# Layer 0 and 1 of a four-layer graph network: products for two output tiles interleaved with the building of the weights, or one output tile at a time, and layer 2 on the same PSUM banks

## The chip, the cores and the metric

The kernel runs on one core of a Trainium2 chip. The metric is the device time of one execution in microseconds. A profile of one execution is beside it: PE is the matrix engine (TensorE), PEld its weight loads, DVE the vector engine, ACT the scalar engine, POOL the GpSimd engine, SP the engine that issues most of the loads.

## The reference

Sixteen graphs of 1024 nodes with 256 features go through four layers. Each layer normalizes the nodes, applies relu, runs a graph layer on the dense 1024 x 1024 adjacency and adds the result to its input. Layer 0 takes its softmax over axis 1, so over the source rows of the weight matrix; layer 1 over axis 2; layer 2 is a mean over neighbours; layer 3 has four heads of width 64.

```python
# layer 0
h = relu(layernorm(x)) @ W
e = leaky_relu(f1[:, :, None] + f2[:, None, :], 0.2)
attention = softmax(where(adj > 0, e, -9e15), axis=1)
x = x + elu(attention @ h)
# layer 1: the same with softmax over axis -1, and f1, f2 from other weights
# layer 2
msg = einsum('bij,biu->bju', adj, h @ W_msg)
x = x + relu(h @ W_upd + msg / deg + bias)
# layer 3: four heads, edge types, softmax over axis -1, relu, a norm over each head
```

## The kernel before, in words

The graph's 1024 nodes are eight tiles of 128 (NT = 8, P = 128). The adjacency is kept as a mask of bytes, written by ACT at line 557 from loads of SP. Most of the matmuls are plain f32; layer 2 takes the adjacency as it is (fp32r) and splits its other operand in a high and a low part (lines 797 and 798), which go through two matmuls (806 and 807).

**Layer 0.** Eight projections (line 632, put out of PSUM by ACT at line 689), then a front of eight steps: in step j DVE makes the weight tile p of 128 x 1024 with two instructions (lines 710 and 712, the second also sums the row into z), a reciprocal (713), and ACT scales the projected tile j by 1/z (714). Then, for each of the eight output tiles i, PE adds up eight products (line 702, called from two places), ACT takes an exp and a copy of it out of PSUM (727 and 729), and DVE adds the result to x (679 and 680). Each second tile also starts the sums for the next layer's norm: shift on DVE (600), hn and squares on ACT (604 and 609), 1/std on POOL (572 and 573), transposes on PE (626) and a copy to ht on ACT (627).

**Early products.** In this kernel the front of layer 0 also takes two of the eight output tiles with it: two PSUM tiles are taken ahead of it, and each step j adds product j to both. Layer 1 does the same (line 751); its front has one DVE instruction a step (758).

**Layer 2.** For each output tile, 16 matmuls add up in one PSUM tile; ACT scales it out of PSUM (812) and copies the degree (813), DVE adds the update term (814) and adds to x (680). The adjacency is loaded from POOL in four blocks of 256 columns through two buffers (565).

**Layer 3** builds its weights on DVE (847) and accumulates on PE (853) in two PSUM tiles for a head, which DVE takes out (861 and 862). A tail on DVE, POOL and ACT (lines 873 to 895) ends the graph.

**PSUM.** There are four pools of two banks each: tr_ps for transposes, mm_ps for projections, at_ps for the output tiles of layers 0 and 1, hd_ps for the output tiles of layer 2 and the heads of layer 3.

**What sets the order.** The graphs are Python generators. Each yields an estimated length after each step, and a queue sorted by due time runs them, the graphs 120 units apart, so that the source traces some two graphs interleaved. A scheduler then orders the instructions of each engine by what is ready by its own estimates and by the free buffers; [...] In the program so ordered, layer 0 of a graph runs beside layer 2 of the graph before it, and layer 1 beside layer 3 of the graph before it.

## Time and profile before

| what | value |
|---|---|
| median of 3 runs | 2985.34 us (2982.68 to 2987.22) |
| the profiled execution | 2987.22 us |
| its span | 2985.3 us |
| PE, PEld busy | 2600.0, 2049.3 us |
| DVE, ACT, POOL busy | 2037.0, 1353.1, 488.4 us |
| line 702 on PE | 2048 rows, 495.5 us |
| line 751 on PE | 2048 rows, 524.1 us |
| lines 806 and 807 on PE | 1024 rows each, 276.3 and 270.8 us |
| mean granted clock of PE | 0.952 |

The span runs from the first to the last instruction. Busy times are sums over an engine's rows; [...] The chain of work that ended last is followed back from the last instruction, at each step to what released it. The stretches quoted below are of one graph's period in the middle of the run, about 1400 to 1582 us.

### The profile page before, as it was taken

Reading aid. Unit: us, or ns where it says so; the run is one execution under the profiler, and the core shown is the slowest. Engines: PE = TensorE matmul, PEld = TensorE weight load, DVE = VectorE, ACT = ScalarE, POOL = GpSimd, SP = SyncE. Lnnn points to the kernel's source line nnn. Section 1 sums busy time; section 2 is a strip of 40 time slices with the busy share of each in tenths; the row PEclk is TensorE's granted clock in tenths of the full one; section 3 lists DMA queues with packets and bytes.
Section 4 is the critical chain, followed back from the end, with each engine's and each line's share of the span. In section 5 each row is a group of like instructions: output and inputs, shape, how many; then the busy total and the mean of one; then the engine's idle time right before and its main releaser. Section 6 shows DMA issues by size and latency. Waiting matters only on the chain.

```text
span 2985.3 us, 62510 instructions
## 1 busy us (share of the span) xinstructions
PE 2600.0 (87%) x25682; PEld 2049.3 (69%) x25682; DVE 2037.0 (68%) x4054; ACT 1353.1 (45%) x3809; POOL 488.4 (16%) x678
## 2 busy tenths in 40 slices
PE   3899898997989979898898989979899798989974
PEld 2767586775767757577676867757677575876754
DVE  3358566686666867667676776867668675776858
ACT  4453554534445444554535544344554435545340
POOL 1010212102121021211202111021211202111011
PEclk8899999999999999999999999999999999999997
DMA  7021321313223131231413223131231313222120
GB/s 229 22 71 37 116 73 62 100 58 108 63 72 99 62 103 51 90 88 62 110 38 113 72 70 94 63 116 51 86 86 66 99 51 100 79 69 78 38 57 31
DMA packets 146070, 233.71 MB, mean 78 GB/s; under 512 B 9392, under 2 KB 94512, under 8 KB 145776
## 3 DMA queue, kind: packets, MB, share of 16 engines
q1 hardware_dynamic: 74608, 145.73, 14.6%
q0 software_dynamic: 71168, 83.89, 11.1%
q8 instruction: 205, 3.36, 0.5%
q14 instruction: 89, 0.73, 0.1%
HBM read 212.35 MB, written 17.24 MB: 77 GB/s over the span
## 4 chain that ended last, share of the span: by engine, by line
PE 49%; DVE 23%; ACT 9%; DMA 7%; issue 6%; POOL 6%; SPq 0%; ACTq 0%; POOLq 0%; DVEq 0%
PE ps_proj L632 14%; PE ps_o L702 12%; PE ps_o L853 11%; PE ps_o L751 7%; DVE p L710 5%; POOL rs L573 5%; DVE p L712 5%; DVE p L847 4%; DMA raw<-in_adj_t 3%; PE pt_h L626 3%; DMA xs<-in_x 3%; ACT mask L557 3%; DVE p L758 2%; ACT hn L604 1%; DVE xs L680 1%
## 5 line engine op out<-in xcount | busy, mean ns | idle before, releaser
L632 PE MATMUL ps_proj<-wx,ht 128*128 128x258 f32 (+2 forms) x2048 | 686.4, 473 | 46.7 <-DVE up L799 34.4
L847 DVE SCALAR_TENSOR_TENSOR p<-row,q,mask 128x1024 f32<-128x1024 f32 x512 | 639.3, 1277 | 71.6 <-PE ps_o L853 46.6
L853 PEld LDWEIGHTS ps_o<-hb,p 128*64 128x64 f32 x16384 | 514.2, 138 | 128.0 <-issue 62.0
L853 PE MATMUL ps_o<-hb,p 128*64 128x65 f32 x16384 | 569.4, 225 | 13.2 <-DVE p L847 7.3
L751 PE MATMUL ps_o<-hs,p 128*128 128x257 f32 x2048 | 524.1, 398 | 41.6 <-DVE p L758 34.6
L702 PE MATMUL ps_o<-hs,p 128*128 128x256 f32 x2048 | 495.5, 387 | 50.6 <-ACT hs L714 40.2
L632 PEld LDWEIGHTS ps_proj<-wx,ht 128*128 128x128 f32 x2048 | 383.2, 203 | 222.8 <-issue 148.6
L702 PEld LDWEIGHTS ps_o<-hs,p 128*128 128x128 f32 x2048 | 378.4, 192 | 119.9 <-ACT hs L714 53.1
L751 PEld LDWEIGHTS ps_o<-hs,p 128*128 128x128 f32 x2048 | 374.8, 194 | 113.5 <-issue 58.3
L572 POOL TENSOR_SCALAR rs<-sq 128x2 f32<-128x2 f32 x192 | 74.2, 387 | 1856.1 <-ACT unread L609 1839.5
L626 PE MATMUL pt_h<-ident,hn 128*128 128x128 f32 x1024 | 189.3, 301 | 141.1 <-ACT hn L604 133.8
L573 POOL TENSOR_TENSOR rs<-rs,neg_half 128x2 f32<-128x2 f32 (+1 forms) x288 | 309.1, 1084 | 16.1
L604 ACT ACTIVATE hn<-xs,shift 128x256 f32<-128x256 f32 x512 | 240.7, 501 | 142.2 <-DVE shift L600 109.9
L807 PE MATMUL ps_o<-lo,adj 128*128 128x258 f32 x1024 | 270.8, 301 | 31.5 <-DVE lo L798 31.5
L774 ACT ACTIVATE e<-ps_o,shares 128x256 f32<-128x256 f32 x128 | 60.0, 469 | 500.2 <-DVE shares L772 500.1
L806 PE MATMUL ps_o<-hi,adj 128*128 128x258 f32 x1024 | 276.3, 306 | 7.6 <-DMA adj<-in_adj 4.3
L626 PEld LDWEIGHTS pt_h<-ident,hn 128*128 128x128 f32 x1024 | 128.1, 151 | 222.2 <-ACT hn L604 164.4
L807 PEld LDWEIGHTS ps_o<-lo,adj 128*128 128x128 f32 x1024 | 196.9, 193 | 43.3 <-DVE lo L798 35.3
L679 DVE SCALAR_TENSOR_TENSOR xs<-e,xs 128x256 f32<-128x256 f32 x256 | 107.8, 421 | 159.3 <-ACT e L727 136.8
L806 PEld LDWEIGHTS ps_o<-hi,adj 128*128 128x128 f32 x1024 | 196.0, 192 | 25.7 <-issue 14.3
L557 ACT ACTIVATE mask<-raw 128x512 uint8<-128x512 int32 x256 | 160.3, 629 | 109.1 <-DVE p L847 64.5
L889 DVE TENSOR_TENSOR res<-res,rs 128x1024 f32<-128x1024 f32 x32 | 39.2, 1225 | 242.3 <-POOL rs L573 242.3
(91 smaller groups left out, 2735.5 us busy)
## 6 DMA issues: line engine op xcount, KB each, us to landing
raw<-in_adj_t SPq DMA_DIRECT2D x256, 256.0 KB
adj<-in_adj POOLq DMA_DIRECT2D x64, 1024.0 KB, 5.9
row<-d_row SPq DMA_DIRECT2D x112, 512.0 KB
xs<-in_x POOLq DMA_DIRECT2D x32, 512.0 KB, 6.1
out<-res SPq DMA_DIRECT2D x32, 512.0 KB
wx<-in_w SPq DMA_DIRECT2D x3, 256.0 KB
d_row<-e_row SPq DMA_DIRECT2D x48, 4.0 KB
wts<-in_w_t SPq DMA_DIRECT2D x2, 256.0 KB
```

The lines of the kernel that those rows point to most:

```text
L557: nc.scalar.activation(self.bytes[:, n, g * HALF : (g + 1) * HALF], raw, AF.Square, accum_out=squares[:, k : k + 1])
L573: nc.gpsimd.tensor_tensor(rs[:, :n], rs[:, :n], neg_half[:, :n], op=OP.pow)
L604: nc.scalar.activation(hn, xs[:, 2 * g + k, :], AF.Relu, bias=shift[:, k : k + 1])
L626: nc.tensor.transpose(pt[:, c, k * P : (k + 1) * P], hn[:, c * P : (c + 1) * P], ident)
L632: nc.tensor.matmul(ps[:, :width], norm.ht[:, c, n * P : (n + 1) * P], wx[:, c, :width], start=(c == 0), stop=(c == DC - 1))
L702: nc.tensor.matmul(ps[:, :D], ps_[j][:, i * P : (i + 1) * P], hs[:, j, :D], start=(j == 0), stop=(j == NT - 1))
L710: nc.vector.scalar_tensor_tensor(p, row_a, q[:, j : j + 1], row_b, op0=OP.mult, op1=OP.max)
L751: nc.tensor.matmul(ps[:, : D + 1], ps_[j][:, i * P : (i + 1) * P], hs[:, j, : D + 1], start=(j == 0), stop=(j == NT - 1))
L806: nc.tensor.matmul(ps[:, : D + 2], a, hi[:, i, : D + 2], start=(i == 0), stop=False)
L807: nc.tensor.matmul(ps[:, : D + 2], a, lo[:, i, : D + 2], start=False, stop=(i == NT - 1))
L847: nc.vector.scalar_tensor_tensor(p, row, q[:, j, h : h + 1], mask[:, j, :], op0=OP.max, op1=OP.mult)
L853: nc.tensor.matmul(pss[g][part, k * HW : (k + 1) * HW], p[:, i * P : (i + 1) * P][:, part], hbv[:, j, h, :], start=(j == 0 and k == 0), st ...
```

## The change

Layers 0 and 1 no longer take two output tiles along their fronts. All output tiles are written as one loop after the front, eight products to a tile, each tile in a PSUM tile of at_ps. Layer 2 takes its PSUM tiles from at_ps in place of hd_ps. Nothing else differs: the same products are added in the same order within each output tile.

```diff
-    EARLY = 2
...
         ps_ = []
-        early = [at_ps.tile([P, HALF], F32, tag="at", name="ps_o0") for _ in range(EARLY)]
-
-        def product(ps, i, j):
-            nc.tensor.matmul(
-                ps[:, :D], ps_[j][:, i * P : (i + 1) * P], hs[:, j, :D], start=(j == 0), stop=(j == NT - 1)
-            )
-
         for j in range(NT):
...
             ps_.append(p)
-            for i, ps in enumerate(early):
-                product(ps, i, j)
             yield 2.6
         for i in range(NT):
-            if i < EARLY:
-                ps = early[i]
-            else:
-                ps = at_ps.tile([P, HALF], F32, tag="at", name="ps_o0")
-                for j in range(NT):
-                    product(ps, i, j)
+            ps = at_ps.tile([P, HALF], F32, tag="at", name="ps_o0")
+            for j in range(NT):
+                nc.tensor.matmul(
+                    ps[:, :D], ps_[j][:, i * P : (i + 1) * P], hs[:, j, :D], start=(j == 0), stop=(j == NT - 1)
+                )
...
```

Layer 1 is changed in the same way (its products are 257 wide and go to ps_o1). In layer 2:

```diff
-            ps = hd_ps.tile([P, HALF], F32, tag="hd", name="ps_o2")
+            ps = at_ps.tile([P, HALF], F32, tag="at", name="ps_o2")
```

## The prediction

> **What bounds the kernel now.** I read the page first: the engines' shares, then the chain that ended last.

> ```profile
> span 2985.3 us, 62510 instructions
> PE 2600.0 (87%) x25682; PEld 2049.3 (69%) x25682; DVE 2037.0 (68%) x4054; ACT 1353.1 (45%) x3809; POOL 488.4 (16%) x678
> ...
> PE 49%; DVE 23%; ACT 9%; DMA 7%; issue 6%; POOL 6%; SPq 0%; ACTq 0%; POOLq 0%; DVEq 0%
> ```

> No engine bounds the whole. The chain goes to and fro between PE (half of it) and the others, so a move is priced where it lands. PE line 702 (layer 0's products) holds 12% of the chain, 11.5% in the finer chain listing: about 340 us, 21 us for each of 16 graphs. Next I took the chain in order of time. The same piece (ACT v L776) comes back at 1417.49 and 1599.68 us: one graph costs 182.2 us. Then I cut one such period into stages by busy time (columns: stretch, its length, then PE, weight loads, DVE, ACT and POOL busy; granted clock, DMA share, GB/s).

> ```profile
> 1455.70:1479.60 23.90, 21.31 (x138) 18.52 (x136) 23.32 (x51) 10.87 (x32) 5.75 (x7) 1.00 0.54 132
> 1479.60:1512.30 32.70, 32.35 (x164) 27.33 (x164) 15.72 (x47) 22.15 (x71) 6.43 (x12) 1.00 0.24 65
> ```

> The first stretch is layer 0's front: DVE builds the eight weight tiles p (lines 710, 712) and is busy 23.32 of 23.90 us. PE's work there is beside the path. The second is the rest of layer 0, and PE is busy 32.35 of 32.70. The chain of this place shows the hand-over (columns: start, us, what):

> ```profile
> 1477.71 1.16 DVE p L712 x2
> 1478.87 0.02 issue
> 1478.89 0.17 DVE z L713
> 1479.07 0.02 issue
> 1479.09 0.52 ACT hs L714
> 1479.61 0.04 issue
> 1479.65 0.71 PE ps_o L702 x2
> 1480.36 0.02 issue
> 1480.38 0.38 ACT e L727
> 1480.77 0.27 ACT v L729
> 1481.04 0.04 issue
> 1481.08 0.70 PE ps_o L702 x2
> 1481.78 0.12 PE ps_o L806
> 1481.90 0.12 PE ps_o L807
> ...
> 1494.46 3.45 PE ps_o L702 x16
> ```

> Until 1478.89 the chain is DVE's. From 1479.65 it is PE's, almost without a gap, to 1532.9. Work done on PE before 1479.6 is free; work done after it is paid in full. How much of layer 0 is done in the free stretch, its instructions on line 702 tell:

> ```profile
> L702 PE MATMUL ps_o<-hs,p x28: 377/379/483, 1460.4 to 1478.4; 128*128 128x256 f32 x28
> ```

> A matmul of the source is two rows here (2048 rows for 16 x 64 calls), so 28 rows are 14 products: weight tiles 0 to 6 into two output tiles. Tile 7's two follow at 1479.65.

> [...] So a product that waits for a p holds all behind it. The trace agrees: 0.38 to 0.85 us of PE idle before line 626 or 702 in the front, with work queued behind. [...] the third output tile waits until 1481.08 for ACT to empty the first.

> **The change part by part.** Arithmetic is the same: every engine has the same kinds and counts of instructions, and SP's queue the same order. Two things move.

> (1) The source no longer interleaves products for two output tiles; (2) layer 2 accumulates in at_ps (two banks) and no longer in hd_ps (two banks). The scheduler orders the engines' instructions itself, so I read the order in the built program. In layer 1's front it still runs two output tiles side by side, although the source no longer says so, and likewise in graph 0's layer 0, where no layer 2 runs. I cost edit (1) by itself at nothing; its cover is the scheduler's choice, and without it eight products of layer 1 would move too. In layer 1 only the second tile's product 4 and an order of 12 and 24 layer 3 products change places (about 0.5 us either way, covered by the six DVE products of line 847 around it).

> In graphs 1 to 15, layer 0 runs beside layer 2 of the graph before, and now both want the two banks of at_ps. The front of the built program: layer 2 tiles 0 to 4; products 0 to 3 into output tile 0 alone; layer 2 tile 5; products 4 to 7; only then layer 2 tile 6, output tile 1 (8 products), layer 2 tile 7, output tile 2 and the rest. Before, layer 2 tiles 0 to 6 and two output tiles lay ahead of that point. (In graphs 1 and 9 to 15 a projection changes place inside the front; what is left for after it is the same.)

> So two pieces leave the covered front for the bare stage:
> - output tile 1: eight products, 16 rows, 3.45 us by the chain's row at 1494.46;
> - layer 2's tile 6: 16 rows of lines 806 and 807 at 0.12 us: 1.92 us.

> Sum 5.37 us. Nothing comes off the path in return: DVE's order up to the last z is unchanged and its 23.3 us of work too, so the front doesn't get shorter. PE's order in the front needs 7 products less 2 to 3 us idle and so has spare time; the adjacency load of tile pair 3 is issued from POOL once tiles 2 and 3 are through (about 1460.5), lands 6.1 us later, and is needed at 1480.

> PSUM waits. After product 7 (ends 1480.1) layer 2 tile 6 needs a bank: either that of output tile 0, emptied by ACT lines 727 and 729 at 1481.04 (the wait which stands there today), or that of layer 2 tile 5, emptied behind them by lines 812 and 813 at about 1481.46. That is 0 to 0.42 us more; I take 0.2. Behind this wait stand all of layer 0's products, so it is paid. The next banks, with ACT in its new order and today's durations: tile 7 of layer 2 needs tile 6 emptied, about 1485.6, and PE comes to it at 1486.5; output tile 2 needs 1487.5, PE comes at 1488.9; output tile 3 needs layer 2 tile 7 emptied, 1491.6, PE comes at 1492.4. All are in time, by 0.7 to 1.4 us; I take 0, the lower bound is 0 too (an earlier bank gives nothing while PE is busy), and the upper bound is one pair of ACT's lines 604 and 609 (0.49 + 0.60 us, twice: 2.2 us).

> The move off hd_ps could save layer 3's waits for its banks: PE line 853 behind DVE lines 861 and 862 is 2.6 + 1.7 us in the whole run, and layer 2's last bank is empty at 1487.2, while layer 3 begins at 1512.3. I take 0, bound -4 us in all. POOL: one adjacency load for the next graph goes behind one more 1/std pair; it is needed some 170 us later. Nothing.

> Everything after 1479.6 (layer 3's rows, layer 1, the norms, the next graph's x into a freed buffer) hangs on this PE stage, so the lag isn't caught up inside a period: 15 x (5.37 + 0.2) = 83.6 us. The profiled execution took 2987.2 us, 1.9 more than its span; so the span is forecast at 3069, that execution at 3071, and against the median of 2985.3 the time is 3069.

> **Rivals.**
> - More PSUM waits. ACT is busy 22.15 of 32.70 us in the bare stage, and layer 2 and layer 0 now alternate on two banks with 0.7 to 1.4 us to spare; a late emptying stops PE. Against it: the order of ACT puts each emptying ahead of its need. Up to 2.2 us a period: 3069 + 15 x 2.2 = 3102.
> - The lag is partly taken up. PE idles 13.5 us between 1411.8 and 1443 in each period, waiting for ACT, POOL and an x load. Were these paced from elsewhere, the lag would shrink there. Against it: the chain runs through these very waits, and the load waits for a buffer released by the late work. Half taken up: 2985 + 42 = 3027; all of it: 2985.
> - Faster. Place: the front. PE waits there for ACT hs L714 and for ACT's lines 813 and 729, 40.2 + 5.8 + 4.6 us in the run, with layer 2 queued behind. If that held back layer 2, and through it DVE's lines 814 and 680 in the front, a front with one product at a time would free DVE: at most 50 us, 2935. It decides if DVE stands idle in the front for more than 5.6 us. It stands idle for 0.6, which is why I hardly believe it.
> - The edit does nothing because the scheduler makes the same order: true of layer 1, but not of layer 0 by the order in the built program.

> **How the numbers follow.** My forecast 0.78 (own range 3055 to 3085: a term of 4.7 to 6.6 us a period); more PSUM waits 0.11 (3085 to 3110); half taken up 0.04 (3005 to 3055); all taken up, within 0.2% (about what a measurement of this kernel can tell from no change, 6 us) 0.03; faster 0.04. Slower is 0.78 + 0.11 + 0.04 = 0.93. The range 3045 to 3105 holds the forecast, most of the PSUM case and the top of the half case.

> **What would show it.** In the changed profile: the period grows from 182.2 to about 187.8 us; DVE stays busy over 95% of a front of about 24 us; 14 rows of line 712 (702 before) in the front in place of 28; 32 layer 2 rows after the last z in place of 16; the bare stage grows from 32.7 to about 38.3 us with PE busy. Wrong would be: PE idle before the layer 2 rows of over 1 us a period (PSUM waits), a period that grows less than the bare stage (the lag is caught up), or a shorter front (the faster rival).

## The result, and the profile after

The changed kernel takes 3108.52 us (median of 4 runs, 3102.31 to 3113.05), the kernel before 2986.28 us beside it: 1.041 times as long, 95% interval 1.0386 to 1.0433. That is 122 us slower, where 84 were forecast. The direction and the place were as predicted, and about two thirds of the size. Most of the missing third lies in something that the prediction gives no price: the clock of TensorE.

From the page of the changed kernel: span, engines, the clock in 40 slices, the chain by engine.

```profile
span 3111.1 us, 62555 instructions
PE 2655.6 (85%) x25682; PEld 2096.9 (67%) x25682; DVE 2048.9 (66%) x4054; ACT 1358.5 (44%) x3809; POOL 482.2 (15%) x678
...
PEclk8999899998999989999899998989999899998997
...
PE 46%; DVE 22%; ACT 12%; DMA 8%; issue 6%; POOL 5%; SPq 0%; ACTq 0%; DVEq 0%; POOLq 0%
```

PE has as many matmuls as before (25682) and is busy 55.6 us longer: the same work ran more slowly. The mean granted clock (the share of its full clock that TensorE was allowed) is 0.931, where it was 0.952. In the row of 40 slices this is hardly to be seen, since each digit is the mean of 78 us.

The stretches that answer to the two of before (length, then PE, weight loads, DVE, ACT and POOL busy; granted clock, DMA share, GB/s), here cut at the first p, the start of the last z and the start of the last row of layer 0's products, so the front is a little shorter than in the prediction's cut:

```profile
1510.85:1534.06 23.21, 18.30 (x108) 15.46 (x106) 23.18 (x50) 10.48 (x31) 6.01 (x6) 0.90 0.56 136
1534.06:1573.93 39.87, 38.14 (x187) 32.76 (x187) 15.20 (x46) 22.22 (x69) 6.31 (x13) 0.93 0.18 47
```

The bare stage of before, cut in the same way:

```profile
1478.89:1511.12 32.23, 31.17 (x157) 26.56 (x158) 14.70 (x47) 21.89 (x69) 7.06 (x13) 1.00 0.25 65
```

The front is bound by DVE as before (23.18 of 23.21 us), and PE does less in it: 18.30 us, where the prediction's line had 21.31. The bare stage behind it is PE's. Both stretches, which ran at a clock of 1.00 before, now have 0.90 and 0.93. The rows of layer 0's products in this front:

```profile
L712 PE MATMUL ps_o<-hs,p x14: 379/379/794, 1522.3 to 1533.4; 128*128 128x256 f32 x14
```

14 rows for 28, as forecast; but the longest takes 794 ns, where the prediction's row had 483. The chain of waits at the hand-over (start, us, what):

```profile
1534.06 0.17 DVE z L705
1534.24 0.02 issue
1534.26 0.52 ACT hs L706
1534.78 0.04 issue
1534.82 1.23 PE ps_o L712 x2
1536.06 0.02 issue
1536.08 0.38 ACT e L716
1536.46 0.27 ACT v L718
1536.73 0.04 issue
1536.78 0.58 PE ps_o L786
1537.36 0.21 PE ps_o L787
...
1539.88 0.12 PE ps_o L787
...
1540.23 3.47 PE ps_o L712 x16
```

Read it against the chain of before, step by step. Product 7's two rows take 1.23 us (0.71 before). Layer 2's tile 6 waits for ACT to empty output tile 0, 0.74 us of PE idle, where output tile 2 waited so before (0.30 us). Then its rows take 0.21 us each until 1539.7, and only then 0.12 as they did before. Output tile 1 follows, 3.47 us for 16 rows, which the prediction had at 3.45. So the moved pieces are there in the order forecast, and the first 5.6 us of the stage run at half clock. In finer stretches of the same place:

```profile
1529.00:1531.00 2.00, 0.83 (x4) 0.38 (x2) 2.00 (x7) 0.01 (x1) 0.00 (x0) 1.00 0.81 197
1531.00:1533.00 2.00, 1.00 (x5) 0.56 (x5) 2.00 (x6) 2.00 (x6) 0.00 (x0) 0.96 1.31 324
1533.00:1535.00 2.00, 1.24 (x3) 0.53 (x4) 1.19 (x3) 1.26 (x4) 1.41 (x2) 0.50 0.02 4
1535.00:1537.00 2.00, 1.26 (x3) 0.54 (x4) 0.42 (x1) 0.92 (x4) 0.00 (x0) 0.50 0.00 0
1537.00:1539.00 2.00, 2.00 (x10) 2.00 (x11) 1.37 (x6) 0.65 (x4) 0.00 (x0) 0.50 0.04 8
1539.00:1541.00 2.00, 2.00 (x13) 1.90 (x12) 0.16 (x1) 1.56 (x6) 0.00 (x0) 0.83 0.00 0
```

From 1529 to 1533 PE is busy 1.83 of 4 us, at the end of the front, where this costs nothing by itself. From about 1532.9 the clock is at 0.50, and it stays there until about 1539.7, well into the stage which PE bounds.

Over the run I cut each of the graphs 1 to 14 at the same three places (the "rest" runs from the last row of layer 0's products to the next graph's first p) and took the means. "Clock time lost" is the length of the stage times one less the granted clock; "PE idle" is the front less PE's busy time in it.

| us a graph | front | bare stage | rest | clock time lost in the bare stage | PE idle in the front |
|---|---|---|---|---|---|
| before | 23.20 | 32.23 | 125.32 | 0.00 | 1.85 |
| after | 23.20 | 40.14 (39.36 to 41.35) | 125.83 | 2.90 (1.71 to 4.33) | 5.32 |

The bare stage grew by 7.91 us. For 15 graphs that is 119 us; the rest's 0.5 us a graph makes about 7 more. Together 126, and the spans differ by 125.8.

### The profile page after: what moved, and what is told of

It reads as the page before. It is cut to its first block, busy times and chain, and to the rows that moved or that the text cites. A ratio compares the mean times of both kernels' runs of the same rounds, so it can differ in the third digit from the quotient of the medians.

```text
span 3111.1 us, 62555 instructions
## 1 busy us (share of the span) xinstructions
PE 2655.6 (85%) x25682; PEld 2096.9 (67%) x25682; DVE 2048.9 (66%) x4054; ACT 1358.5 (44%) x3809; POOL 482.2 (15%) x678
## 4 chain that ended last, share of the span: by engine, by line
PE 46%; DVE 22%; ACT 12%; DMA 8%; issue 6%; POOL 5%; SPq 0%; ACTq 0%; DVEq 0%; POOLq 0%
PE ps_proj L631 14%; PE ps_o L833 11%; PE ps_o L712 9%; PE ps_o L746 7%; DVE p L702 5%; POOL rs L572 5%; DVE p L704 4%; DVE p L827 4%; DMA xs<-in_x 3%; ACT mask L556 3%; DMA raw<-in_adj_t 3%; PE pt_h L625 2%; ACT unread L608 2%; ACT hn L603 2%; DVE p L740 2%
## 5 line engine op out<-in xcount | busy, mean ns | idle before, releaser
L746 PE MATMUL ps_o<-hs,p 128*128 128x257 f32 x2048 | 521.1, 397 | 43.2 <-DVE p L740 36.2
L712 PE MATMUL ps_o<-hs,p 128*128 128x256 f32 x2048 | 501.1, 393 | 41.1 <-ACT hs L706 41.1
L712 PEld LDWEIGHTS ps_o<-hs,p 128*128 128x128 f32 x2048 | 391.4, 197 | 106.1 <-ACT hs L706 56.5
L746 PEld LDWEIGHTS ps_o<-hs,p 128*128 128x128 f32 x2048 | 374.0, 193 | 114.9 <-issue 60.8
L786 PE MATMUL ps_o<-hi,adj 128*128 128x258 f32 x1024 | 306.9, 330 | 55.3 <-DMA adj<-in_adj 40.4
L787 PE MATMUL ps_o<-lo,adj 128*128 128x258 f32 x1024 | 300.3, 324 | 31.6 <-DVE lo L778 31.5
L786 PEld LDWEIGHTS ps_o<-hi,adj 128*128 128x128 f32 x1024 | 223.6, 219 | 78.9 <-issue 42.6
L787 PEld LDWEIGHTS ps_o<-lo,adj 128*128 128x128 f32 x1024 | 224.9, 220 | 43.1 <-DVE lo L778 35.5
```

The costliest lines, as they stand in the source:

```text
L712: nc.tensor.matmul(ps[:, :D], ps_[j][:, i * P : (i + 1) * P], hs[:, j, :D], start=(j == 0), stop=(j == NT - 1))
L746: nc.tensor.matmul(ps[:, : D + 1], ps_[j][:, i * P : (i + 1) * P], hs[:, j, : D + 1], start=(j == 0), stop=(j == NT - 1),)
L786: nc.tensor.matmul(ps[:, : D + 2], a, hi[:, i, : D + 2], start=(i == 0), stop=False)
L787: nc.tensor.matmul(ps[:, : D + 2], a, lo[:, i, : D + 2], start=False, stop=(i == NT - 1))
```

## The experiments

Two theories stood at the start. **Clock** (theory A): with 14 rows gone from the front, PE idles there and its clock is halved, which is paid behind the front. **Banks** (theory B): layer 2 and layer 0 now share two PSUM banks, and the waits for them are what costs more than forecast. In the kernels with a scrap product, everything that the changed kernel computes is still computed; the extra products go to a PSUM tile that nobody reads.

**Part (1) of the change alone.** The loops of the source as changed, layer 2 back in hd_ps:

```diff
-            ps = at_ps.tile([P, HALF], F32, tag="at", name="ps_o2")
+            ps = hd_ps.tile([P, HALF], F32, tag="hd", name="ps_o2")
```

> Only the loops are changed: no early tiles in the source of layers 0 and 1, layer 2 stays in hd_ps. Theory (the loss comes from the banks that layers 0 and 2 now share; the scheduler runs two output tiles side by side by itself where both at_ps banks are free): 28 rows of layer 0's products in the front as before, 2980 to 2992 us. Rival (the early tiles in the source carry the gain): about 3100 us.

Measured: 2987.52 us, ratio 0.9992 (0.9983 to 1.0002), so no change that can be told. From the list of one tile's instructions in one front of this kernel:

```profile
L712 PE MATMUL ps_o<-hs,p x28: 377/379/484, 1455.0 to 1472.3; 128*128 128x256 f32 x28
```

28 rows are in the front, though the source says "one output tile at a time": the scheduler runs two tiles side by side where two banks are free. The bare stage is 32.23 us, that of before. So the loops alone cost nothing, and the loss comes when layer 2's move to at_ps is added to them. (The opposite, the move with the early tiles kept, wasn't tried; by the source, layer 2 would have to wait there for banks that the early tiles hold along the front.)

**Scrap products in the front.** The changed kernel, with one product into a scrap tile of hd_ps at each of the eight steps:

```diff
+        scrap = hd_ps.tile([P, HALF], F32, tag="hd", name="ps_scrap")
...
             ps_.append(p)
+            nc.tensor.matmul(
+                scrap[:, :D], p[:, P : 2 * P], hs[:, j, :D], start=(j == 0), stop=(j == NT - 1)
+            )
```

> The changed kernel, and in each step of layer 0's front one more product of the new weight tile, into an hd_ps bank that nobody reads: PE's front is as full as before the change, but the bare stage still has the 5.4 us of moved work and the same two banks. Theory A (the part of the loss above 5.4 us a graph is TensorE's clock, which falls to half when PE idles in the front): the clock stays at 1.0 in front and bare stage, the bare stage falls from 40.1 to about 38 us, the time to 3070 to 3085 us. Theory B (that part is waits for the two shared banks): no change, 3103 to 3113 us.

Measured: 3083.25 us (3078.02 to 3091.98), ratio 1.0321 (1.0298 to 1.0345). More work on PE made the kernel some 27 us faster (0.0089 of 2986 by the ratios). The bare stage of one graph:

```profile
1518.89:1557.41 38.52, 36.79 (x188) 31.67 (x189) 15.21 (x46) 22.12 (x69) 6.30 (x13) 1.00 0.18 47
```

The clock is 1.00, and the stage takes 38.52 us in all ten graphs where it is; in the other five the clock fell and it takes 39.3 to 40.8. The mean of graphs 1 to 14 is 38.92 us, 1.22 less than in the changed kernel. The banks are the same as in the changed kernel, and so is layer 2's wait for them (0.7 us a graph). Banks alone can't explain a difference that goes away by adding work.

**The same without product 7, and only late.** In the experiment above, scrap product 7 stands ahead of the true product 7 on PE, at the beginning of the bare stage. Here it is left out, and so are those of steps 0 to 3:

```diff
-            nc.tensor.matmul(
-                scrap[:, :D], p[:, P : 2 * P], hs[:, j, :D], start=(j == 0), stop=(j == NT - 1)
-            )
+            if 4 <= j < NT - 1:
+                nc.tensor.matmul(
+                    scrap[:, :D], p[:, P : 2 * P], hs[:, j, :D], start=(j == 4), stop=(j == NT - 2)
+                )
```

> The changed kernel with the scrap products of steps 4, 5 and 6 alone (1.3 us of PE work a graph, ahead of product 7, so that nothing on the path waits for them). Theory A, with PE's idle time just ahead of the bare stage as the trigger: the clock still falls in the middle of the front (after the wait for the adjacency load), where it costs nothing, but not in the bare stage: about 38 us for that stage, 3075 to 3085 us. If the idle time in the middle of the front is the trigger, or the clock isn't the cause: 3095 to 3113 us.

Measured: 3080.73 us (3075.16 to 3085.14), ratio 1.0308 (1.0288 to 1.0328). This kernel holds the cleanest comparison, two graphs of one execution with the same instructions:

```profile
1709.96:1749.55 39.59, 37.86 (x186) 32.79 (x187) 15.50 (x47) 22.23 (x69) 6.30 (x13) 0.96 0.28 76
1895.37:1933.45 38.08, 36.35 (x187) 31.29 (x188) 15.26 (x47) 22.11 (x69) 6.30 (x13) 1.00 0.28 72
```

One lost 1.5 us to the clock, the other none. Nine graphs of 15 take 38.08 to 38.10 us at full clock; five lose 1.71 us of clock time and take 39.59 to 39.64; one lies between. So 38.09 us is what the stage takes with the moved work and the shared banks at full clock: 5.86 more than before, against the 5.37 forecast for the work, and some 0.5 for waiting. (The changed kernel itself has no graph at full clock; its graphs that lose 1.71 us take 39.36 to 39.60, near the 39.59 to 39.64 here.) The product left out is the difference to the first scrap kernel: 38.52 - 38.09 = 0.43 us.

**Why one graph and not the other.** Every change of the granted clock in this trace lies on one grid of 3.413 us from the first record of the clock to the last: cut on it, all 901 stretches are at 1.00 or at 0.50, none between. The same graphs, cut on that grid at their hand-over:

```profile
1708.97:1712.38 3.41, 1.83 (x8) 0.97 (x8) 1.54 (x4) 2.11 (x8) 1.41 (x2) 1.00 1.36 303
1712.38:1715.79 3.41, 3.41 (x17) 3.41 (x17) 1.37 (x6) 1.54 (x6) 0.00 (x0) 0.50 0.03 5
```

```profile
1893.29:1896.70 3.41, 2.11 (x9) 1.14 (x8) 2.21 (x6) 2.27 (x7) 1.45 (x3) 1.00 0.98 244
1896.70:1900.11 3.41, 2.67 (x20) 2.50 (x20) 1.80 (x7) 1.90 (x7) 0.00 (x0) 1.00 0.34 68
```

PE has the same three gaps in both graphs: 0.45 us ahead of scrap product 6, 0.84 (0.85 in graph 10) ahead of product 7, 0.74 ahead of layer 2. In graph 9 the second and the third fall into one stretch: PE is busy 3.41 - 0.84 - 0.74 = 1.83 us, 0.54 of it, and the next stretch, full of work, runs at half clock. In graph 10 the boundary lies between them: busy for 0.62 of the first and 0.78 of the second, and the clock stays. PE's rows in the two bare stages are the same, in the same order. The changed kernel on its own grid:

```profile
1529.43:1532.84 3.41, 1.23 (x6) 0.40 (x4) 3.41 (x11) 1.85 (x6) 0.00 (x0) 1.00 1.23 303
1532.84:1536.26 3.42, 2.44 (x4) 1.00 (x4) 1.35 (x5) 1.60 (x5) 1.41 (x2) 0.50 0.03 5
1536.26:1539.67 3.41, 2.89 (x13) 2.89 (x14) 1.79 (x7) 2.06 (x7) 0.00 (x0) 0.50 0.02 5
1539.67:1543.08 3.41, 3.41 (x19) 3.06 (x18) 0.86 (x3) 1.24 (x6) 1.09 (x2) 1.00 0.00 0
```

Busy for 1.23 of 3.41 us, 0.36: the clock falls in the next stretch. That one is busy for 0.71, and the one after it is at 0.50 too; behind that one, busy for 0.85, the clock is at 1.00 again. A whole stretch at half clock loses 1.71 us; of these two, 0.61 us is lost ahead of the last z, and 2.80 in the bare stage. So the loss differs between graphs with the same instructions, by where the gaps lie against the grid.

**Layer 0's first tile in another bank.** The changed kernel, output tile 0 of layer 0 in hd_ps, so that layer 2 has both banks of at_ps during the front:

```diff
-            ps = at_ps.tile([P, HALF], F32, tag="at", name="ps_o0")
+            ps = (hd_ps if i == 0 else at_ps).tile([P, HALF], F32, tag="hd" if i == 0 else "at", name="ps_o0")
```

> The changed kernel, with layer 0's first output tile in hd_ps, so that layer 2 has both at_ps banks in the front again. Seven of layer 2's tiles fit in the front as before; output tile 1 stays behind it. By the moved work alone 15 x 3.45 = 52 us over before: 3038 us. By theory A PE idles about 4.8 us in the front and the clock may still fall, which adds up to 2 us a graph: 3038 to 3068 us. By theory B (waits for banks) nothing is added: 3038 us at most.

Measured: 3097.67 us (3093.82 to 3100.41), ratio 1.0361 (1.0341 to 1.0381). My expectation missed: tile 6 of layer 2 did go back into the front (16 rows behind the last z, not 32), and yet the bare stage takes 39.36 us, 0.8 less than in the changed kernel. What was gained in work was lost in clock. PE on the timeline, with the idle time before each row in brackets, and the stretches of the grid (cut some 0.05 us late, hence 0.99 and 0.51):

```profile
1522.71 0.84 PE L625 MATMUL pt_h<-ident,hn 128*128 128x128 f32 x4 [2.02 <-ACT hn L603]
1524.00 0.76 PE L712 MATMUL ps_o<-hs,p 128*128 128x256 f32 x2 [0.45 <-ACT hs L706]
1525.98 1.22 PE L712 MATMUL ps_o<-hs,p 128*128 128x256 f32 x2 [1.22 <-ACT hs L706]
1528.36 1.22 PE L712 MATMUL ps_o<-hs,p 128*128 128x256 f32 x2 [1.16 <-ACT edges L793]
```

```profile
1521.15:1524.56 3.41, 1.40 (x6) 0.70 (x6) 3.41 (x9) 2.41 (x8) 0.02 (x1) 0.99 0.49 112
1524.56:1527.97 3.41, 1.42 (x3) 0.50 (x2) 1.10 (x4) 1.58 (x5) 1.39 (x2) 0.50 0.00 0
1527.97:1531.38 3.41, 3.02 (x7) 2.48 (x8) 2.12 (x10) 2.34 (x9) 0.00 (x0) 0.51 0.00 0
```

With layer 2 done earlier, PE has nothing to do but wait for the front's last steps: 2.02 + 0.45 + 1.22 us idle around the end of the front (the last of them reaches 0.76 us into the bare stage), and 3.68 us of clock time lost in the bare stage on average (2.90 in the changed kernel). I had put the clock at up to 2 us a graph and waits for banks at nothing; the next run shows about 2.8 for the first and 0.9 for the second. It is the same kernel with the gap filled.

**The same with scrap products 0 to 6.** The last edit, with the scrap tile of the first scrap kernel at `j < NT - 1`:

> Layer 0's first output tile in hd_ps, and the scrap products of steps 0 to 6 beside it: only the eight products of output tile 1 are still behind the front. Theory A with additive parts: bare stage 32.2 + 3.45 + about 0.5 us of waits = 36.2 us, 3040 to 3052 us, against 3098 us without the scrap. If the 3.7 us over the moved work in the run without the scrap are waits for banks: 3090 us or more.

Measured: 3051.98 us (3048.10 to 3055.66), ratio 1.0219 (1.0202 to 1.0236): 7 more products a front (14 rows), none of use, and some 42 us less (by the two ratios). The bare stage at full clock, as ten of the graphs have it:

```profile
1503.05:1539.65 36.60, 34.43 (x170) 29.36 (x171) 14.99 (x46) 22.36 (x69) 6.13 (x13) 1.00 0.16 47
```

36.60 is 32.23 + 3.45 for output tile 1 + 0.92. Most of the 0.92 is one wait for a bank, 1.16 us for ACT's `edges` (line 793 in the kernel without scrap, where the same wait stands), in place of the 0.30 that the kernel before has behind product 7. This tells the two terms of the forecast apart: with tile 6 back in the front, tile 1 alone remains. And 39.36 - 36.60 = 2.76 us is what the clock costs a graph without the scrap. (One graph takes 38.44 us at full clock; only 8 rows of layer 0's products are in its front, where the others have 12 or 14.)

**A version that might win.** Before the change too, the clock is at half for part of the time: 7.07 us of clock time a graph in the rest, next to PE's wait for ACT hn near the end of layer 1. In the kernel before I put 12 scrap products (257 wide) behind layer 1's last output tile, to keep the clock through that wait:

```diff
+            if i == NT - 1:
+                scrap = hd_ps.tile([P, HALF], F32, tag="hd", name="ps_scrap")
+                for w in range(12):
+                    nc.tensor.matmul(
+                        scrap[:, : D + 1], ps_[w % NT][:, i * P : (i + 1) * P], hs[:, w % NT, : D + 1],
+                        start=(w == 0), stop=(w == 12 - 1),
+                    )
```

> The kernel before, with 12 more products behind layer 1's last output tile, into an hd_ps bank that nobody reads: 5.2 us of PE work where PE idles 7.2 us and its clock falls to half (0.50 from 1417 to 1423 us). Theory A: the transposes and projections after it run at full clock, 2 us a graph less, 2950 to 2960 us. Rival (this place is paced by ACT, POOL and DVE, or the added rows come before the work that matters): no gain or a loss, 2980 to 3030 us.

Measured: 3030.91 us (3030.40 to 3033.22), ratio 1.0139 (1.0122 to 1.0156). No gain but a loss, just above the upper end of what the rival had (3030). PE's timeline at that place:

```profile
1438.29 0.69 PE L626 MATMUL pt_h<-ident,hn 128*128 128x128 f32 x2 [6.74 <-ACT hn L604]
1438.77 2.78 PE L773 MATMUL ps_scrap<-hs,p 128*128 128x257 f32 x6
...
1441.77 2.29 PE L773 MATMUL ps_scrap<-hs,p 128*128 128x257 f32 x8
```

The scheduler spread the scrap among the transposes: of its 24 rows 10 came ahead of the wait that they were to fill and 14 behind it, where they stand before the projections. The wait takes 6.74 us, where it took 7.24. Clock time lost in the rest fell only from 7.07 to 5.97 us, and the rest grew by 2.67. So the filling took 0.50 us off the wait, and its place in the source didn't decide where on PE it came.

## Why the prediction was right and wrong

**Right.** The front stays with DVE: 23.20 us before and after. Tile 1 and layer 2's tile 6 leave it: 14 rows for 28 in it, 32 layer 2 rows for 16 behind it. Their price is 5.37 us a graph, and a bare stage at full clock is 5.86 longer. Edit (1) by itself is worth nothing, by the scheduler's choice. The lag isn't taken up in the rest, which didn't get shorter. Later waits for banks were taken at nothing, and the list of waits has just one on layer 2's rows, of 0.6 us, in the whole run. Neither the "half taken up" nor the "faster" rival has anything to show.

**Wrong: the step "PE's order in the front needs 7 products less 2 to 3 us idle and so has spare time".** It gave PE's idle time in the front a price of nothing, and took every duration behind it from a trace at full clock. PE idles 5.32 us in the front after the change (1.85 before), part of it in the last 5 us, and in each of the 15 graphs the clock falls to half around the last z, between 2.2 us ahead of it and 2.2 us behind it, for two or three stretches of the grid in 12 of them and one in three. That costs 40.14 - 38.09 = 2.05 us a graph, some 31 of the 42 us between the forecast of 3069 and the span of 3111.1 (the wait below makes 4 more, the rest 7). The profile of before had what it takes. Cut on its own grid, at the end of its front:

```profile
1474.86:1478.28 3.42, 2.25 (x11) 1.33 (x10) 3.42 (x9) 2.46 (x8) 0.07 (x1) 1.00 0.37 98
1478.28:1481.69 3.41, 2.26 (x10) 1.28 (x9) 1.53 (x7) 2.11 (x7) 1.34 (x2) 1.00 0.00 1
```

PE was busy for 0.66 of both, and the clock stayed. In this same trace no stretch with less than 0.45 kept the full clock. Two products of tile 1 less in the first, 0.43 us each, leave 2.25 - 0.86 = 1.39 us, so by this estimate 0.41, about the 0.36 that the changed kernel then showed.

**Mis-sized: the wait for a bank after product 7,** taken at 0.2 from a range of 0 to 0.42. Measured as what is left in the bare stage at full clock: 38.09 - 32.23 - 5.37 = 0.49 us. In the list of waits (sum, count, longest) the changed kernel has

```profile
PE ps_o L786 <- ACT v L718: 11.1, 15, 0.7
```

and the kernel before, at the same place,

```profile
PE ps_o L702 <- ACT v L729: 4.6, 15, 0.3
```

so 0.74 us for 0.31: 0.43 more, just above the top of the range. The 0.49 is 0.29 us a graph more than forecast, 4 us in all. (The stage also has a new wait of 0.22 us for ACT hn, at the transposes of line 625; how much of the 0.49 is due to it isn't shown.)

**Not foreseen, and without a price: another adjacency load.** The prediction's load, that of tiles 6 and 7, was in time: tile 6 waits for ACT alone. But PE now waits for the load ahead of it, that of tiles 4 and 5, in the front: 2.50 us up to 1518.91 in the graph shown (40.4 us in 16 waits over the run, 4.3 before). Before, two products for each of the two early tiles stood ahead of tile 4 on PE and filled this time; now the products stand behind it. The clock falls there too, to 0.50 until 1522.6, and nothing is late for it, since DVE bounds the front to its end.

**The PSUM rival had nearly the right total (3102) for the wrong reason.** It asked for up to 2.2 us a graph of waiting for banks, and put as its sign a PE idle by more than 1 us before the layer 2 rows. The idle time is 0.74, and a kernel with the same banks and more work on PE is faster.

**Open.** The rest is 0.5 us a graph longer in the changed kernel and 0.5 to 0.9 shorter in the three kernels with scrap in layer 0's front than it was before. So the mean bare stages account for 18 of the 27 us that the first scrap kernel gains on the changed one, for 24 of the 31 of the late one, and for 34 of the 42 between the two kernels with the other bank; each time 7 or 8 us remain. Single graphs differ by 4 to 9 us in the rest within each run, and I give these about 7 us no cause.

## What to carry to other kernels

Idle time of TensorE was not free here although another engine bounded the stage: with a PE-bound stage right behind it, the idle time decided the clock at which that stage began (40.14 us with 5.32 us idle in the front, 38.09 at full clock with scrap products there). When work leaves PE, work out from the trace how busy PE stays in each stretch of the clock's grid (3.413 us here) around the start of the next PE-bound stage, and price the stretch that follows at half clock where too little is left (in these traces the clock always fell below 0.41, and never above 0.59). The grid didn't start anew with a stage: the same order of instructions took 39.59 us in graph 9 of the late scrap kernel and 38.08 in graph 10. Whether two accumulations ran side by side was decided here by the banks they could get and not by the loops of the source; ask of a shared pool what it lets the scheduler interleave.

## What the runs showed of the hardware that I had not expected

Stretches at half clock in a whole execution: 84 before, 126 after, 79 for part (1) alone, 98 and 87 for the two scrap kernels (late, and all eight), 114 for the other bank, 80 for that with scrap. Their order is not that of the times, since the moved work is paid as well; but the changed kernel, with 42 more than before, lost 42 x 1.71 = 72 us more of clock time, of which some 43 (15 x 2.90) in the bare stages. The remainder lies in the fronts: 1.98 us of clock time a graph (mean of graphs 1 to 14, none before), some 30 in all. It cost nothing, since DVE bounds the front, which takes 23.20 us in both kernels.
